# A graph layer, a linear-attention mixer and sixteen experts on one core: the experts' buffers moved, two additions moved to VectorE, one load moved

## The chip, the cores and the metric

The kernel runs on one core of a Trainium2 chip. The metric is device time in microseconds (us) of one execution. A core has five engines that run side by side, each through its own instructions in order: TensorE (PE, with its weight loads shown as PEld), VectorE (DVE), ScalarE (ACT), GpSimd (POOL) and SyncE (SP). Here SP does nothing but issue DMAs and load registers for them; POOL issues the indirect DMAs (gathers and scatters by a list of rows) beside additions of its own. All data is float32.

## The reference, cut to what matters

```python
xn = _layernorm(x)                                   # x: 3125 x 256
x = x + gnn(xn, edge_attr_3, src, dst, ...) + mix(xn, ...)
x = x + ffn(_layernorm(x), ...)

# gnn: 100000 edges
tmp = relu(concat(h[src], w) @ W1.T + b1)            # summed into the rows dst
h_lin = relu(concat(h, h_N) @ W2.T);  return h_lin / max(norm(h_lin), 1e-12)

# mix: 4 layers
h = layernorm(x);  x = x + linear_attn(h) 
h = layernorm(x);  x = x + (gelu(h @ W1 + b1) @ W2 + b2)

# ffn: 16 experts, the best 2 of each node
topk_vals, topk_idx = top_k(x @ gate_w + gate_b, 2);  topk_w = softmax(topk_vals)
h = relu(x @ w1[e] + b1[e]);  o = h @ w2[e] + b2[e]  # 256 -> 512 -> 256
y = x + sum_k topk_w[k] * o[topk_idx[k]];  return layernorm(y) * gamma + beta
```

## The kernel before, in words

The 3125 nodes are 25 tiles of 125 rows, in seven blocks (five of four tiles, one of three, one of two; `BLOCKS`, `NB` = 7). The running x of all nodes stays in SBUF as `xm`. The program has these stages:

1. The graph's edges and the first three mixer layers, interleaved, to about 1350 us.
2. The last mixer layer (from L1138). For each block `b`: `stage_f1` (first half), `stage_y(b+1)`, `stage_ln2(b+1)`, `add_update(b+1)`, `stage_yn(b-1)`, `stage_f1` (second half), `stage_g(b+2)`, `stage_yT(b-1)`, `stage_f2` (first pair of tiles), `stage_logits(b-1)`, `stage_t2(b+1)`, `stage_f2` (second pair), `stage_ranks(b-1)`, `stage_stats(b)`. `stage_ln2` normalizes a block into `xh` on DVE and then adds the bias `b2` to `xm` on POOL (L667). `add_update` loads the block's x into `xr` (SP), adds it to `xm` on POOL (L740), and then adds the normalized graph update to `xm` on DVE (L744). `stage_f2` adds the second product to `xm` on DVE (L700). `stage_yn` writes the experts' input of a block to the DRAM table `ynodes` (SP), and adds `beta` to `xm` on POOL (L1077). `stage_logits` and `stage_ranks` choose two experts for each node (DVE `lg`, `gate`, `sel`; PE `l_ps`, `rank_ps`), and eight scatters per block of four tiles (POOL, L1131) write each node into a slot of its expert in the DRAM table `slots`.
3. The first four expert tiles (`early`). They are full tiles of 256 slots that are known three blocks before the end of the layer. Their buffers lie in the memory of `hNT` and `qT`, which this layer no longer needs: `ew` (two sets of expert weights, written as `hNT<-ffn_w`), `ygT`, `yg` (the gathered rows, L140), `hs`, `o`. Their gathers are called for at b = NB - 2 (`e_nodes`), their products run between and behind the last block's stages, and their results are scattered into the DRAM table `outs` (L211).
4. The experts' phase (from L1215). Pools of SBUF are opened and closed like a stack; the new pools `big2`, `wts2` and `tmp2` take the place of the closed `big`, `wts` and `tmp`. `big` held `qT`, `hNT`, two `xh1`, `msum` and two `kmax`, in this order; `big2` holds `ogs` (51,200 bytes per partition), `gamma` and `eps`; `wts2` four weight buffers `ew` and six `yg`; `tmp2` `ids`, `ygT`, `hs`, `hb`, `o`. `run_tiles` goes through 33 tiles, 16 of them of 128 slots and 17 of 256, nearly in turn. For each tile: `load_slots` (SP: `ids<-slots`, L1241, some with an expert's number from a register), `load_weights` (SP: `ew<-ffn_w`, L147, 1.15 MB), `load_nodes` (POOL: `yg<-ynodes`, L140), `stage_t` (PE transposes L157, ACT copy L159), `stage_e1` (PE L167 or L175), `stage_ht` for small tiles, `stage_e2` (PE L204, DVE L208 and L209, POOL scatter L211). Loads of slots run six tiles ahead, weights and nodes three.
5. Two branches for tiles beyond these, and the output stage (from L1301): SP loads the results of all nodes from `outs` into `ogs` with 32 DMAs; PE sums each node's two rows, ACT and DVE normalize, DVE multiplies by `gamma` (L1341) and adds `xm` (L1342), POOL's queue stores.

What sets the order of an engine's instructions: in `tc.manual_schedule(engines=...)` the engines named keep the order of the program, and a scheduler orders the others by its own estimate of when each instruction is ready. In the first three layers these are PE, ACT and POOL; in the last layer PE and ACT (`in_order - {Pool}`); in `run_tiles` PE and ACT. So the order on SP, POOL and DVE in stages 2 to 4 is the scheduler's. It may also lift an instruction that stands behind the branches in the program over them, if nothing ties it to them: `eps` (L1303) is set before the experts' phase.

Of the kernel before, what the change touches and what calls it, by code (L numbers as in the profile page):

```python
# [8 lines left out]
F32 = mybir.dt.float32  # L9
# [8 lines left out]
D = 256  # L18
P = 128
TP = 125  # L20
# [35 lines left out]
def rows_bcast(ap, parts):  # L56

    return bass.AP(tensor=ap.tensor, offset=ap.offset, ap=[[0, parts], [1, ap.shape[-1]]])
# [7 lines left out]
def gps_layer(ctx: ExitStack, tc: tile.TileContext, a, out):  # L66
    nc = tc.nc
# [4 lines left out]
    def by_parts(queue, dst, src):  # L72

        for p in (slice(0, TP // 16 * 16), slice(TP // 16 * 16, TP)):
            queue.dma_start(dst[p], src[p])  # L75

    def by_tile(rows):

        return rows.rearrange("(p t) d -> p t d", t=NT)
# [28 lines left out]
    def rsqrt(dst, v, u):  # L108

        nc.vector.tensor_scalar(u.bitcast(I32), v.bitcast(I32), 1, None, op0=ALU.logical_shift_right)  # L110
        nc.vector.tensor_scalar(dst.bitcast(I32), u.bitcast(I32), -1.0, float(0x5f3759df),
                                op0=ALU.mult, op1=ALU.add)
        for _ in range(3):
            nc.vector.scalar_tensor_tensor(u, v, -0.5, dst, op0=ALU.mult, op1=ALU.mult)
            nc.vector.tensor_mul(u, u, dst)  # L115
            nc.vector.scalar_tensor_tensor(dst, u, 1.5, dst, op0=ALU.add, op1=ALU.mult)

    def finish_stats(r):
        rs = slice(r[0], r[-1] + 1)
        nc.vector.tensor_scalar(rs_v[:, rs], mv[:, rs, 1], EPS, None, op0=ALU.add)  # L120
        rsqrt(rstd[:, rs], rs_v[:, rs], rs_u[:, rs])

    def normalize(dst, src, t):
        nc.vector.tensor_scalar(dst, src, mv[:, t, 0:1], rstd[:, t:t + 1],
                                op0=ALU.subtract, op1=ALU.mult)
# [94 lines left out]
    with ExitStack() as ph:  # L220
        big = ph.enter_context(tc.tile_pool(name="big", bufs=1))
# [187 lines left out]
        NB = len(BLOCKS)  # L409
# [9 lines left out]
        def worked(columns, mark=None):  # L419


            nonlocal place
            if not spread or held:
                return
            place += columns * (NG + 1 + LEAD) / total
            while due and due[-1][0] <= place:
                _, kind, step, i = due.pop()
                if kind == 0 and mark is not None:
                    nc.gpsimd.tensor_copy(tick, mark)
                    mark = None  # L430
                step(i)
# [76 lines left out]
        def stage_stats(b):  # L508
            for t in BLOCKS[b]:
                stats(tmp, xm[:, t, :], t)  # L510
# [135 lines left out]
        def stage_y(l, b):  # L646
            for t0, o, n in pairs(b):
                ps = mm_tile("y_ps")[:TP].rearrange("p (i d) -> p i d", d=D)
                for i in range(n):
                    for c in range(KC):  # L650
                        nc.tensor.matmul(ps[:, i, :], qT[:, c, cols(t0 + i)], mo[:, c, :],  # L651
                                         start=(c == 0), stop=(c == KC - 1))
                xs = xm[:, t0:t0 + n, :]
                nc.vector.tensor_add(xs, xs, ps[:, :n, :])
                for t in range(t0, t0 + n):
                    stats(tmp, xm[:, t, :], t)
                worked(n * KC * D, xm[:1, t0, :1])

        def stage_ln2(b):
            r = BLOCKS[b]  # L660
            finish_stats(r)
            xh = tmp.tile([TP, BT, D], F32, name="xh")
            st["xh", b] = xh
            for i, t in enumerate(r):
                normalize(xh[:, i, :], xm[:, t, :], t)
            xs = xm[:, r[0]:r[-1] + 1, :]
            nc.gpsimd.tensor_add(xs, xs, b2[:TP, None, :].to_broadcast([TP, len(r), D]))  # L667

        def stage_t2(l, b):
            h2T = tmp.tile([P, KC, BT * TP], F32, name="h2T")  # L670
# [33 lines left out]
        def load_update(b):  # L704
            r = BLOCKS[b]
            n = len(r)
            xnT = tmp.tile([P, KC, BT * TP], F32, tag="hT", name="xnT", bufs=2)
            nc.sync.dma_start(xnT[:, :, :n * TP], xnT_d[:, :, cols(r[0], n)])
            hl = tmp.tile([TP, BT, D], F32, tag=("qs", "ek")[b % 2], name="hl")
            ss = tmp.tile([TP, 3, BT], F32, name="ss", bufs=2)  # L710
            st["update", b] = xnT, hl, ss
# [18 lines left out]
                                                   op1=ALU.mult, accum_out=ss[:, 0, i:i + 1])  # L730


        def add_update(b):
            r = BLOCKS[b]
            n = len(r)
            _, hl, ss = st.pop(("update", b))
            xr = tmp.tile([TP, BT, D], F32, tag="ekT", name="xr")
            by_parts(nc.sync, xr[:, :n, :], xv[:, r[0]:r[-1] + 1, :])
            xs = xm[:, r[0]:r[-1] + 1, :]
            nc.gpsimd.tensor_add(xs, xs, xr[:, :n, :])  # L740
            nc.vector.tensor_scalar(ss[:, 0, :n], ss[:, 0, :n], 1e-24, None, op0=ALU.max)
            rsqrt(ss[:, 1, :n], ss[:, 0, :n], ss[:, 2, :n])
            for i, t in enumerate(r):
                nc.vector.scalar_tensor_tensor(xm[:, t, :], hl[:, i, :], ss[:, 1, i:i + 1], xm[:, t, :],  # L744
                                               op0=ALU.mult, op1=ALU.add)
# [3 lines left out]
        def start_layer(l):  # L749
            nonlocal b2  # L750
            load(l, "Wo", "W1", "W2")
            b2 = tmp.tile([P, D], F32, name="b2")
            nc.sync.dma_start(b2, rows_bcast(a["mix_b2"][l], P))
# [384 lines left out]
        with tc.manual_schedule(engines=in_order - {mybir.EngineType.Pool}):  # L1138
            start_layer(last)
            load_update(0)  # L1140
            load_update(1)

            def worked(columns, mark=None):
                pass

            context(last, [lambda: stage_q(last, NB - 1), lambda: stage_g(0, slice(0, 1)),
                           lambda: stage_g(0, slice(1, 2)), lambda: stage_g(1, slice(0, 1))])
            stage_y(last, 0)
            stage_qT(last, NB - 1)
            stage_ln2(0)  # L1150
            add_update(0)
            stage_g(1, slice(1, 2))
            stage_t2(last, 0)
            stage_y(last, 1)
            for b in range(NB):
                stage_f1(last, b, range(0, NF // 2))
                if 0 < b < NB - 1:
                    stage_y(last, b + 1)
                if b + 1 < NB:
                    stage_ln2(b + 1)  # L1160
                    add_update(b + 1)
                if b == NB - 2:
                    for x in early:
                        e_nodes(x)
                if b > 0:
                    stage_yn(b - 1)
                stage_f1(last, b, range(NF // 2, NF))
                if b + 2 < NB:
                    load_update(b + 2)
                    stage_g(b + 2)  # L1170
                if b > 0:
                    stage_yT(b - 1)
                stage_f2(last, b, slice(0, 1))
                if b > 0:
                    stage_logits(b - 1)
                if b + 1 < NB:
                    stage_t2(last, b + 1)
                stage_f2(last, b, slice(1, 2))
                if b > 0:
                    stage_ranks(b - 1)  # L1180
                stage_stats(b)
                if b == NB - 3:
                    early_loads(BLOCKS[b][0])
            stage_yn(NB - 1)
            e_t(early[0])
            e_1(early[0])
            stage_yT(NB - 1)
            e_2(early[0], 0)
            stage_logits(NB - 1)
            e_t(early[1])  # L1190
            e_2(early[0], 1)
            stage_ranks(NB - 1)
            e_weights(early[2])
            e_1(early[1])
            for i in range(1, NFE):
                e_2(early[i], 0)
                if i + 1 < NFE:
                    e_t(early[i + 1])
                e_2(early[i], 1)
                if i + 2 < NFE:  # L1200
                    e_weights(early[i + 2])
                if i + 1 < NFE:
                    e_1(early[i + 1])
# [11 lines left out]
    with ExitStack() as ph:  # L1215
        big = ph.enter_context(tc.tile_pool(name="big2", bufs=1))
# [7 lines left out]

        ogs = big.tile([TP, K, NT, D], F32, name="ogs")
        gamma = big.tile([P, D], F32, name="gamma")
        nc.sync.dma_start(gamma, rows_bcast(a["ffn_gamma"], P))

        which_e, first, rest, loaded = [], [], [], set()

# [69 lines left out]

        ov = by_tile(out)  # L1301
        eps = big.tile([TP, 1], F32, name="eps")
        nc.vector.memset(eps, EPS)  # L1303
        ends = [1, 3, 7, 11, 15, 19, 23, NT]
        parts = [range(i, j) for i, j in zip([0] + ends, ends)]
# [110 lines left out]
```

## Time and profile before

| | us |
|---|---|
| median of 3 runs | 1956.14 (1951.93 to 1962.21) |
| the profiled execution | 1949.88 |
| its span, first to last instruction | 1948.2 |
| PE busy | 1808.2 (93%) |
| DVE busy | 1164.5 (60%) |
| POOL busy | 1117.7 (57%) |
| ACT busy | 749.0 (38%) |
| mean granted TensorE clock | 0.965 |
| last product of the first four expert tiles starts, ends | 1675.99, 1677.98 |
| first transposes of the experts' phase | 1691.08 |
| last product of the experts' phase ends | 1887.7 |
| output loads issued | 1897.95 to 1920.5 |

In the lines of the profile, a line begins with the engine (SPq is SP's queue) and names the line of the kernel, then output<-inputs by the program's names and the shape. Times are us from the start of the span. "<-" behind an idle time names what ended it; "issue" there means that the profile shows nothing that the engine waited for.

### The profile page before, as it was taken

To read this page: it belongs to the slowest core of one execution; us is meant where nothing else is said; L and a number is where in the kernel's file an instruction comes from. 1 tells how busy PE (TensorE), PEld (TensorE's weight loads), DVE (VectorE), ACT (ScalarE), POOL (GpSimd) and SP (SyncE) were. 2 spreads that over 40 slices of the span, in tenths; PEclk is the share of its full clock that TensorE was granted. 3 is DMA by queue.
4 is the path that set the end of the run, shared out by engine and by line. 5 is a ranking of instruction groups with operands and counts; after the bars stand their busy time and mean duration, and the time that the engine had idled before them with its cause. 6 is when DMAs were issued, how large, how long until landed. Compare 5 with 4: busy or idle time off the path is not lost. (4 is left out here: it accounts for less than half of the span.)

```text
span 1948.2 us, 28580 instructions
## 1 busy us (share of the span) xinstructions
PE 1808.2 (93%) x8965; PEld 1225.3 (63%) x8965; DVE 1164.5 (60%) x3727; ACT 749.0 (38%) x1352; POOL 1117.7 (57%) x1414
## 2 busy tenths in 40 slices
PE   6989999999989999999889999998899998799975
PEld 4865655666656566656555555666677777588862
DVE  7654666766665776666655666774546664233336
ACT  3532454444534444554233554443222232122222
POOL 1005788888828788888267888881113446355521
PEclk8998999999999999999889999999999999899997
DMA  6212333333513333334323333333211003577746
GB/s 173 91 52 68 97 107 103 103 102 106 150 52 102 95 103 104 106 101 125 90 77 88 102 103 105 103 108 95 91 41 27 20 17 109 182 266 277 268 146 196
DMA packets 95088, 216.64 MB, mean 111 GB/s; under 512 B 26760, under 2 KB 53391, under 8 KB 90192
## 3 DMA queue, kind: packets, MB, share of 16 engines
q0 software_dynamic: 45904, 121.36, 21.6%
q1 hardware_dynamic: 49024, 93.34, 15.0%
q8 instruction: 77, 1.26, 0.3%
q14 instruction: 83, 0.68, 0.1%
HBM read 192.20 MB, written 22.35 MB: 110 GB/s over the span
## 5 line engine op out<-in xcount | busy, mean ns | idle before, releaser
L348 POOL DMA_INDIRECT gat<-proj,src_i x784 | 760.1, 970 | 190.0 <-issue 142.3
L685 PE MATMUL f_ps<-h2T,ww 128*128 128x500 f32 (+2 forms) x896 | 369.5, 561 | 7.2 <-ACT h2T L442 6.2
L695 PE MATMUL f_ps<-ww,gT 128*125 128x256 f32 x1600 | 362.9, 382 | 0.1
L392 ACT ACTIVATE gat<-gat 128x512 f32<-128x512 f32 x392 | 239.2, 630 | 308.5 <-DVE gat L391 291.6
L391 DVE TENSOR_TENSOR gat<-gat,pw 128x512 f32<-128x512 f32 x392 | 250.6, 677 | 171.8 <-PE pw L386 156.6
L695 PEld LDWEIGHTS f_ps<-ww,gT 128*125 128x125 f32 x1600 | 294.2, 187 | 70.7 <-issue 21.5
L685 PEld LDWEIGHTS f_ps<-h2T,ww 128*128 128x128 f32 x896 | 169.5, 196 | 184.7 <-issue 130.2
L687 ACT ACTIVATE gT<-f_ps,ffb 128x500 f32<-128x500 f32 (+2 forms) x224 | 135.6, 632 | 139.3 <-PE f_ps L685 138.8
L667 POOL TENSOR_TENSOR xm<-xm,b 125x1024 f32<-125x1024 f32 (+2 forms) x28 | 59.6, 2129 | 137.2 <-DVE rs_u L115 57.0
L372 PE MATMUL pq<-gat,hot 128*32 128x256 f32 x1568 | 121.9, 388 | 9.1 <-ACT gat L392 8.7
L366 DVE TENSOR_TENSOR hNT<-hNT,win_ps 128x64 f32 x392 | 84.2, 215 | 72.4 <-PE win_ps L363 62.7
L386 PE MATMUL pw<-w1w,ea 8*128 8x512 f32 x784 | 121.0, 644 | 0.8 <-DVE qs L568 0.6
L1131 POOL DMA_INDIRECT slots<-rec,at x50 | 59.8, 1196 | 102.9 <-DVE rs_u L115 63.8
L700 DVE TENSOR_TENSOR xm<-xm,f_ps 125x512 f32<-125x512 f32 (+1 forms) x52 | 34.6, 666 | 133.9 <-PE f_ps L695 133.9
L598 PE MATMUL m_ps<-xh,ek 125*128 125x257 f32 x400 | 96.6, 394 | 5.4 <-ACT ek L584 5.4
L651 PE MATMUL y_ps<-mo,qT 128*125 128x256 f32 x400 | 98.9, 402 | 0.8 <-DVE mo L641 0.8
L561 PE MATMUL q_ps<-wwq,hT 128*125 128x256 f32 x400 | 94.5, 387 | 4.7 <-DVE gat L391 2.9
L211 POOL DMA_INDIRECT outs<-o,ids x50 | 49.5, 989 | 84.7 <-DVE o L209 83.6
L204 PE MATMUL e_ps<-ew,hs 128*128 128x256 f32 x400 | 97.2, 380 | 0.5 <-DVE o L208 0.3
L535 PE MATMUL k_ps<-hT,wwk 128*128 128x500 f32 (+2 forms) x224 | 92.6, 556 | 4.9 <-DVE hT L444 4.2
L651 PEld LDWEIGHTS y_ps<-mo,qT 128*125 128x125 f32 x400 | 77.9, 200 | 23.8 <-issue 5.7
L91 DVE BATCH_NORM_STATS2 bnst<-xm 125x6 f32<-125x256 f32 x225 | 88.7, 414 | 4.8 <-DMA xm<-x 2.8
(268 smaller groups left out, 2585.6 us busy)
## 6 DMA issues: line engine op xcount, KB each, us to landing
ew<-ffn_w SPq DMA_DIRECT2D x33, 1154.0 KB
gat<-proj,src_i POOLq DMA_INDIRECT x784
ww<-mix_W SPq DMA_DIRECT2D x8, 1024.0 KB
ea<-ea_g SPq DMA_DIRECT2D x98, 64.0 KB
hNT<-ffn_w SPq DMA_DIRECT2D x4, 1154.0 KB
ogs<-outs SPq DMA_DIRECT2D x10, 448.0 KB
xnT_d<-stage SPq DMA_DIRECT2D x5, 500.0 KB
xnT<-xnT_d SPq DMA_DIRECT2D x5, 500.0 KB
```

Of the source, the lines that this page charges most:

```text
L204: nc.tensor.matmul(ps[:, j, :], x["hs"][:, f, j * P:(j + 1) * P], x["w2"][:, f, :], start=(f == 0), stop=(f == NEF - 1))
L348: nc.gpsimd.indirect_dma_start(out=gats[-1][:, (j // SC) % 2, j % SC, :], out_offset=None, in_=proj, in_offset=bass.IndirectOffsetOnAxis(a ...
L372: nc.tensor.matmul(pq[s * W:(s + 1) * W, :], hot[:, s * SC + i, :], gats[s // 2][:, s % 2, i, :], start=(i == 0), stop=(i == SC - 1))
L386: nc.tensor.matmul(pws[s], ea[s * W:s * W + SC * 4, :], w1w[s * W:s * W + SC * 4, :], start=True, stop=True)
L391: nc.vector.tensor_add(msg, msg, pws[s])
L392: nc.scalar.activation(msg, msg, AF.Relu)
L561: nc.tensor.matmul(ps[:, i, :], hT[:, c, cols(o + i)], wt["Wq"][:, c, :], start=(c == 0), stop=(c == KC - 1))
L598: nc.tensor.matmul(ps, st["ek", b][:, i, c * P:(c + 1) * P], xh1s[b % 2][:, i, :], start=(i == 0), stop=(i == n - 1))
L651: nc.tensor.matmul(ps[:, i, :], qT[:, c, cols(t0 + i)], mo[:, c, :], start=(c == 0), stop=(c == KC - 1))
L685: nc.tensor.matmul(ps, wt["W1"][:, c, f * P:(f + 1) * P], st["h2T", b][:, c, :m], start=(c == 0), stop=(c == KC - 1))
L687: nc.scalar.activation(gT[:, f, :m], ps, AF.Gelu, bias=ffb[:, l, f:f + 1])
L695: nc.tensor.matmul(ps[:, i, :], st["gT", b][:, f, cols(o + i)], wt["W2"][:, f, :], start=(f == 0), stop=(f == NF - 1))
```

## The change

Three edits. `stage_ln2` and `add_update` get an argument for the engine that adds the bias `b2` and the block's x to `xm`; it is POOL as before, but DVE for the last block (`b + 2 == NB`). In `big2` a tile `room` of 2304 floats per partition (9,216 bytes) is laid out behind `gamma`; nothing reads or writes it, and all that is laid out after it lies so much higher. The load of `gamma` moves from the start of the experts' phase to the start of the output stage, behind the branches in the program.

```diff
-        def stage_ln2(b):
+        def stage_ln2(b, adder=nc.gpsimd):
...
-            nc.gpsimd.tensor_add(xs, xs, b2[:TP, None, :].to_broadcast([TP, len(r), D]))
+            adder.tensor_add(xs, xs, b2[:TP, None, :].to_broadcast([TP, len(r), D]))
...
-        def add_update(b):
+        def add_update(b, adder=nc.gpsimd):
...
-            nc.gpsimd.tensor_add(xs, xs, xr[:, :n, :])
+            adder.tensor_add(xs, xs, xr[:, :n, :])
...
                 if b + 1 < NB:
-                    stage_ln2(b + 1)
-                    add_update(b + 1)
+                    adder = nc.gpsimd if b + 2 < NB else nc.vector
+                    stage_ln2(b + 1, adder)
+                    add_update(b + 1, adder)
...
         gamma = big.tile([P, D], F32, name="gamma")
-        nc.sync.dma_start(gamma, rows_bcast(a["ffn_gamma"], P))
+        big.tile([P, 2304], F32, name="room")
...
         eps = big.tile([TP, 1], F32, name="eps")
+        nc.sync.dma_start(gamma, rows_bcast(a["ffn_gamma"], P))
         nc.vector.memset(eps, EPS)
```

## The prediction

> **What bounds the kernel now.** The page's first part gives TensorE (PE) 93% of the span, so only what makes PE wait, or run slowly, costs time:
>
> ```profile
> PE 1808.2 (93%) x8965; PEld 1225.3 (63%) x8965; DVE 1164.5 (60%) x3727; ACT 749.0 (38%) x1352; POOL 1117.7 (57%) x1414
> ```
>
> Next the waits of the stretch 1600 to 1700 us, which holds the end of the last mixer layer, the first four expert tiles and the start of the experts' phase (columns: total, times, longest, in us):
>
> ```profile
> PE ygT_ps L157 <- issue: 13.1, 1, 13.1
> DVE xm L744 <- POOL xm L740: 12.2, 1, 12.2
> ...
> POOL yg L140 <- DMA ids<-slots: 10.0, 1, 10.0
> ...
> PE rank_ps L1119 <- DVE sel L1104: 6.2, 2, 4.0
> ```
>
> PE has two holes: 13.1 us ahead of the experts' first transposes, 4.0 us ahead of a rank product. For the first I read the timelines of PE, SP and POOL around it (start, duration, work, idle time before and its releaser):
>
> ```profile
> 1675.99 1.99 PE L204 MATMUL e_ps<-hNT,qT 128*128 128x256 f32 x8 [0.52 <-DVE qT L208]
> 1691.08 0.66 PE L157 MATMUL ygT_ps<-ident,yg 128*128 128x128 f32 x2 [13.10 <-issue]
> ...
> 1703.20 1.88 PE L167 MATMUL e_ps<-ew,ygT 128*128 128x512 f32 x4
> ...
> 1714.65 1.88 PE L167 MATMUL e_ps<-ew,ygT 128*128 128x512 f32 x4
> ```
>
> ```profile
> 1664.34 2.01 SPq L1241 DMA_DIRECT2D ids<-slots  x3
> 1681.92 0.34 SPq L1227 DMA_DIRECT2D gamma<-ffn_gamma  x1
> 1682.31 2.32 SPq L147 DMA_DIRECT2D ew<-ffn_w  x3
> ```
>
> ```profile
> 1671.43 0.97 POOL L211 DMA_INDIRECT outs<-qT,ids  x1 [1.54 <-DVE qT L209]
> ...
> 1679.24 0.97 POOL L211 DMA_INDIRECT outs<-qT,ids  x1 [1.54 <-DVE qT L209]
> 1682.70 0.99 POOL L140 DMA_INDIRECT yg<-ynodes,ids  x1 [2.49 <-issue]
> ```
>
> SP issues nothing from 1666.35 to 1681.92, then gamma and at once the experts' weights; POOL's gathers `yg` start at the same moment. The DVE timeline says what let go:
>
> ```profile
> 1600.55 1.16 DVE L124 TENSOR_SCALAR xh<-xm,mv,rstd 125x256 f32<-125x256 f32 x2
> 1613.92 0.88 DVE L744 SCALAR_TENSOR_TENSOR xm<-hl,ss,xm 125x256 f32<-125x256 f32 x2 [12.22 <-POOL xm L740]
> ...
> 1681.99 0.06 DVE L1303 MEMSET eps<- 125x1 f32 x1 [3.03 <-DMA outs<-qT,ids]
> ```
>
> `eps`, in the same new pool as gamma, waited for the landing of the last scatter that reads `qT`, so that scatter, issued at 1679.24, frees pool `big`. The sizes agree: `big` holds 25,024+25,280+2x4,128+2,080+64 = 60,704 B per partition, the new `big2` only 51,200+1,024+32 = 52,256. The next pool (`wts2`: `ew`, `yg`) begins inside the old `big`, on `xh1`, whose readers ended long before. That it waited all the same means the wait goes by whole pools. `ids`, laid wholly over the old `tmp`, went out at 1664.34.
>
> For the second hole, PE's timeline and windows with the granted clock (busy by engine, PEclk, DMA share, GB/s):
>
> ```profile
> 1610.38 3.62 PE L695 MATMUL f_ps<-ww,gT 128*125 128x256 f32 x16
> 1617.99 0.43 PE L1119 MATMUL rank_ps<-sel,earlier 125*125 125x64 f32 x2 [3.99 <-DVE sel L1104]
> ```
>
> ```profile
> 1619.00:1623.00 4.00, 3.78 (x11) 3.05 (x11) 3.72 (x24) 2.11 (x3) 3.09 (x3) 0.57 0.39 108
> 1650.00:1653.00 3.00, 1.43 (x9) 1.03 (x8) 2.90 (x11) 0.69 (x2) 2.34 (x3) 1.00 0.04 1
> 1653.00:1657.00 4.00, 4.00 (x13) 3.22 (x12) 2.64 (x16) 0.47 (x1) 2.75 (x3) 0.57 0.77 264
> ...
> 1691.00:1698.00 7.00, 6.32 (x15) 3.40 (x16) 0.05 (x1) 1.57 (x3) 0.52 (x1) 0.52 0.99 395
> ```
>
> DVE stood 12.2 us behind the last block's additions, which POOL had put between its gathers and scatters. Behind them on DVE were `lg` and the chain to `sel`, for which PE waited. Each hole is followed by PE at about half clock.
>
> **Change, part 1: the buffers.** With `room` `big2` is 52,256+9,216 = 61,472 B, 768 more than `big`, so `wts2` begins past it and waits only for the old `wts` and `tmp`. Their last readers are the second f2 product of the last block and its statistics, by 1638.4. SP then goes from `ids` (end 1666.35) to the three weights. From the first such issue (1682.31) to the end of POOL's wait for the next `ids`, queued behind them (1697.48), was 15.2 us, so all three land by 1681.6, and the first needs less: its product began 10.0 us after its issue, so by 1676.4.
>
> PE can't start before the PSUM of the four tiles is read: DVE's last L208 runs 1678.02 to 1678.44, so 1678.6 instead of 1691.08, 12.5 us earlier. Then the clock. From the first transposes to the third tile's product took 1703.20-1691.08 = 12.1 us, against a full-clock period of 11.45. The first pair lacks the previous tile's e2 (2 x 1.73) and has about 1.1 us of transposes and copy and 0.75 of uncovered `hb` copy: 11.45-3.46+1.85 = 9.8. That is 2.3 more, 14.8 in all.
>
> Two deductions. The gathers: the early `ids` let POOL go 2.5 us after their issue (1606.68 to 1609.15), so `yg` issues at 1669, or at about 1673 behind the scatter of 1671.43. Under the weights' traffic it took 8.4 us to PE's start; the last early gather (1620.55) had landed when SP wrote `ynodes` at 1623.42, 2.9 us. So `yg` is ready between 1672 and 1681.4, PE up to 2.8 us late; I take 0.6, nearer to the early end, since the weights have a head start. The clock: a gap of about a microsecond remains. The rows show half clock (0.57) after a stretch with 1.43 of 3.00 us busy and no idle piece over 1.6 us. A half-clock stretch as in the row 1619 to 1623 costs 4.00 x 0.43 = 1.7; I take half of it, 0.85. [...] Part 1: -14.8+0.6+0.85 = -13.3, bounds -10.3 and -14.8.
>
> **Part 2: DVE adds.** No 125x512 addition of two SBUF tiles on DVE stands here; the nearest, gamma's product and the addition of x in the output stage, take 0.69 (L1341, L1342 at 512). Two are 1.4, on DVE that is idle from 1601.71 until f2's first PSUM at about 1608.5: hidden; uncovered, 1.4. The load of `xr` was issued at 1573.24. `lg` then runs at 1610.3 instead of 1615.3, `sel` ends by 1613, and PE goes from f2's end (1614.0) to the ranks: 3.99 saved. The half-clock stretch after the hole goes too, 1.7: -5.7. Bounds -4.0 (clock unchanged) and -6. POOL loses 2 x 1.29 us between its gathers, so it isn't late next: its next scatters could start at 1619.2, and their ranks are ready by 1617.2. Everything after is chained to these ranks and moves along.
>
> [...]
>
> **Part 3: gamma.** Its issue costs SP 0.34. Ahead of the 32 output loads (22.55 us, 0.70 each, which pace the output) it adds 0.34; if the scheduler lifts it over the branches, as it does with `eps`, nothing, since SP has little to issue until the first weight buffer comes free at about 1687. Its 128 KB at 269 GB/s delay the loads by 0.5 at most. I take +0.3.
>
> **Sum.** -13.3-5.7+0.3 = -18.7. The profiled execution took 1949.88 (span 1948.2), so 1931.2. The median of the runs is 6.3 above that execution: 1956.1-18.7 = 1937.4.
>
> **Rivals.**
> A. *POOL's order.* If the scheduler puts the fourth tile's gathers ahead of the last early scatters, POOL stands until those `ids`, behind three weights, are there (1681.6); two gathers later, at 1684.1, the scatter starts and lands 2.7 us on or more, and `eps`, still waiting for it, holds DVE to 1687 or 1690, while the first expert relu is wanted at 1683. Or the first gathers come after the last scatter (1680.5). For: POOL's order is the scheduler's, `eps` stood there before. Against: those `ids` are issued after the weights. Costs 6: 1943. Chance 0.13.
> B. *The buffers aren't freed*, because the wait doesn't go by pools as I read it. Only part 2 stays: 1956.1-5.4 = 1950.7. For: it is inferred from one wait. Against: `ids` went early. 0.10.
> C. *DVE adds bring nothing*, since the scheduler places them late on DVE or another wait follows: 1943. For: DVE's order is the scheduler's too. Against: it is idle there. 0.09.
> D. *Slower: SP's order.* Freed early, the experts' weights may be queued ahead of the weights of the third and fourth early tile (third issued at 1652.94, wanted at 1662.20). It decides when four loads, with the one whose expert comes from the tile list (ready at 1663.44), stand ahead. From about 1658.3 (both moved by part 2) three loads take 15.2 and two more 3.45 each (1.18 MB at the 343 GB/s of 1682.3 to 1697.5), 22.1 in all: 1680.4 against 1656.5 wanted. Early tiles end 23.9 later, at 1696.2, with a half-clock stretch at 1698; experts start at 1698.7 against 1691.1, less 2.3 for the faster first pair, +0.3 for gamma: +5.6, so 1961.7. Against: the third tile's weights are ready 10 us before the list. 0.06.
>
> **How the numbers follow.** My forecast has 0.62. A measurement tells about 0.5% (9.8 us) from no change. Faster by more: 0.61 of the forecast, 0.10 of A, 0.08 of C: 0.79. Within: the rest of A and C, most of B, half of D: 0.15. Slower: half of D and what I haven't seen: 0.06. The range runs from the full bounds (-14.8-6, 1935, less 5 for the scatter of the runs shown) to B: 1930 to 1950.
>
> **What would show it.** Right: SP issues `ew` within 3 us of the first `ids`, or even before; PE's hole before L157 `ygT_ps<-ident,yg` falls from 13.1 to under 3; PEclk is near 1.0 there; L744 no longer waits for POOL; the rank's 4.0 goes. `eps` still waits for the last scatter. Wrong: SP still stands until the last scatter lands (B), DVE stands at `eps` while PE waits (A), or L175 `e_ps<-hNT` waits for a DMA (D).

## The result, and the profile after

The changed kernel takes 1938.8 us (median of 6 runs, 1930.3 to 1941.2) where the kernel before takes 1953.4 beside it: ratio 0.9914, 95% interval 0.9885 to 0.9943, so 11 to 22 us faster. Run once more beside the kernel before (`after_again` below) it came to 1933.9 against 1954.2, ratio 0.9896 (0.9875 to 0.9918). The forecast was 1937.4, in a range of 1930 to 1950, from a gain of 18.7; the gains measured are 14.6 and 20.3.

The profiled execution is one of 1941.19 us with a span of 1939.5, only 8.7 below that of before. That difference is not the change's size. PE runs the same 8965 matmuls in the same order in both kernels, so each can be set beside its twin. The matmul that starts at 1577.49 before starts at 1585.03 after: this execution was 7.5 us late when it came to the first changed instruction, through more stretches at half clock in stages that are the same in both (49.5 us lost to half clock up to there, 41.0 before). Below, a time "from the mark" is counted from this matmul, and a gain is the difference of two such times.

| start of, us from the mark | before | after | gain | after_again |
|---|---|---|---|---|
| first rank product (last but two block) | 40.50 | 36.35 | 4.15 | 36.35 |
| second products of the last but one block | 50.55 | 44.62 | 5.93 | 44.62 |
| next rank product | 61.07 | 56.15 | 4.92 | 56.38 |
| last early tile's second products | 95.98 | 92.20 | 3.78 | 92.46 |
| first transposes of the experts' phase | 113.60 | 97.28 | 16.32 | 97.54 |
| third tile's first product | 125.72 | 106.96 | 18.76 | 107.22 |
| last matmul of the program | 351.44 | 334.10 | 17.34 | 333.87 |

The page's first part, and what is left on PE of the waits of 1590 to 1700 us (total, times, longest):

```profile
PE 1813.0 (93%) x8965; PEld 1227.6 (63%) x8965; DVE 1170.0 (60%) x3729; ACT 748.2 (39%) x1352; POOL 1114.6 (57%) x1412
```

```profile
PE rank_ps L1119 <- DVE sel L1104: 4.9, 2, 3.2
...
PE ygT_ps L157 <- issue: 0.6, 1, 0.6
```

The 13.1 us ahead of `ygT_ps` are 0.6, DVE's 12.2 at L744 are gone from the list, and `rank_ps` keeps 4.9, now ahead of another product. PE's timeline after (start, duration, work, idle time before and its releaser):

```profile
1621.38 0.33 PE L1119 MATMUL rank_ps<-sel,earlier 125*125 125x64 f32 x2
...
1641.18 0.65 PE L1119 MATMUL rank_ps<-sel,earlier 125*125 125x48 f32 x2 [3.23 <-DVE sel L1104]
...
1643.82 5.23 PE L175 MATMUL e_ps<-hNT 128*128 128x256 f32 x16 [0.69 <-ACT hNT L159]
...
1682.31 0.41 PE L157 MATMUL ygT_ps<-ident,yg 128*128 128x128 f32 x2 [0.56 <-issue]
1683.32 1.98 PE L167 MATMUL e_ps<-ew,ygT 128*128 128x512 f32 x4 [0.60 <-ACT ygT L159]
```

The first rank product now has no idle time before it. The second one waits longer than before (3.23, was 2.23), and the first early product behind it takes 5.23 where the same product later takes 3.62. At the boundary the transposes start 0.56 us behind the last early product (which ran from 1679.76 to 1681.76).

SP's queue after, and POOL's:

```profile
1641.12 0.36 SPq L147 DMA_DIRECT2D ew<-ffn_w  x1
...
1668.11 1.97 SPq L1244 DMA_DIRECT2D ids<-slots  x3
...
1705.74 0.36 SPq L1306 DMA_DIRECT2D gamma<-ffn_gamma  x1
```

```profile
1638.42 1.81 POOL L1077 TENSOR_TENSOR xm<-xm,beta 125x768 f32<-125x768 f32 x1
...
1673.96 0.99 POOL L140 DMA_INDIRECT yg<-ynodes,ids  x1 [0.30 <-PE e_ps L204]
...
1683.01 0.98 POOL L211 DMA_INDIRECT outs<-qT,ids  x1 [0.77 <-DVE qT L209]
```

The first experts' weight now goes out at 1641.12, 42 us before the last early scatter (1683.01), ahead even of the last two early tiles' weights (`hNT<-ffn_w`, from 1656.80); two more follow at 1670.98. The gathers `yg` stand between early scatters. gamma's load was lifted over the branches, as `eps` is, and goes out 23 us into the experts' phase.

### The profile page after: what moved, and what is told of

It reads as the page before. It is cut to its first block, busy times and chain, and to the rows that moved or that the text cites. A ratio compares the mean times of both kernels' runs of the same rounds, so it can differ in the third digit from the quotient of the medians.

```text
span 1939.5 us, 28572 instructions
## 1 busy us (share of the span) xinstructions
PE 1813.0 (93%) x8965; PEld 1227.6 (63%) x8965; DVE 1170.0 (60%) x3729; ACT 748.2 (39%) x1352; POOL 1114.6 (57%) x1412
## 5 line engine op out<-in xcount | busy, mean ns | idle before, releaser
L700 DVE TENSOR_TENSOR xm<-xm,f_ps 125x512 f32<-125x512 f32 (+1 forms) x52 | 34.7, 667 | 135.7 <-PE f_ps L695 132.6
```

## The experiments

Nine of the twelve kernels ran on three chips on which the kernel before takes 2194 to 2199 us, the last three on one with 1954. Nearly all of that difference lies ahead of the mark (at 1818 to 1830 us there, 1577 in the profile of before): up to there PE stands 195 to 207 us on those chips and 82 on the quicker ones, and loses 128 to 147 us to half clock against 31 to 50. What makes it is not shown. Each kernel is therefore set against the kernel before on its own chip, and the traces from the mark on.

| run | this, us | before, us | ratio, 95% interval | idle ahead of the first transposes, us |
|---|---|---|---|---|
| buffers_only | 2187.8 | 2199.1 | 0.9942 (0.9922 to 0.9963) | 1.21 |
| buffers_only_2 | 2185.9 | 2194.4 | 0.9949 (0.9922 to 0.9975) | 0.56 |
| adds_only | 2196.2 | 2199.1 | 0.9986 (0.9968 to 1.0004) | 12.91 |
| adds_only_2 | 2196.6 | 2194.4 | 0.9995 (0.9970 to 1.0019) | 12.86 |
| room_2104 | 2194.3 | 2199.1 | 0.9986 (0.9965 to 1.0007) | 13.51 |
| room_2112 | 2183.9 | 2199.1 | 0.9929 (0.9911 to 0.9946) | 0.56 |
| gamma_first | 2185.3 | 2197.1 | 0.9955 (0.9931 to 0.9980) | 0.56 |
| gamma_moved | 2196.6 | 2197.1 | 1.0001 (0.9974 to 1.0028) | 13.21 |
| beta_dve | 2182.0 | 2197.1 | 0.9926 (0.9898 to 0.9954) | 0.84 |
| after_again | 1933.9 | 1954.2 | 0.9896 (0.9875 to 0.9918) | 0.56 |
| late_rank | 1941.2 | 1954.2 | 0.9919 (0.9894 to 0.9944) | 3.43 |
| late_rank_beta | 1934.7 | 1954.2 | 0.9914 (0.9891 to 0.9937) | 2.54 |

### One part at a time

The buffers and gamma without the additions:

```diff
-                    adder = nc.gpsimd if b + 2 < NB else nc.vector
+                    adder = nc.gpsimd
```

> The buffer and gamma as in the changed kernel, the last block's two additions back on POOL. My theory: the two holes are separate, so PE's hole ahead of the experts' first transposes (13.1 us before, 0.6 after) stays under 1.5, DVE's 12 us wait at L744 and PE's 4.0 at the rank product come back, and the whole is 13 to 16 us faster than before, 2 to 4 us slower than the changed kernel. Rival, the additions did it (POOL, freed of 2.6 us, let its gathers and the weights go early): the hole stays above 8 us and the whole is less than 6 us faster than before.

The additions without the buffers:

```diff
-        big.tile([P, 2304], F32, name="room")
+        nc.sync.dma_start(gamma, rows_bcast(a["ffn_gamma"], P))
...
-        nc.sync.dma_start(gamma, rows_bcast(a["ffn_gamma"], P))
```

> The two additions on DVE alone, no room, gamma loaded at the start of the experts' phase as before. My theory: the 4.0 us wait at the rank product goes, and with what the next blocks give back the last early product comes 3 to 6 us earlier; the hole of 13 us ahead of the experts' first transposes stays within 2 us of 13, so the whole is 3 to 6 us faster than before. Rival, POOL's queue held the experts' weights: the hole falls below 5 and the whole is over 12 us faster.

The buffers bring 11 to 13 us of the chip's 15.6 (`room_2112`, next section): 0.9942 is 12.8 us of 2199. This is slightly below the 13 expected, and the hole is closed as expected. The additions bring 3.1 (interval -0.9 to 7.0), the lower end of what was expected and not clear of nothing, with the hole as it was. Both were run again on another of these three chips:

> [...] If the additions bring nothing (what is gained at the rank is given back on every chip), it is within 2 us of before.

> The buffers (and gamma) alone beside it. If the two parts simply add up to the changed kernel's 17 to 20 us: 13 to 16 faster than before. If the additions' part needs the buffers' or the other way round, the two gains sum to 3 us or more away from it.

There the additions bring nothing that can be measured (0.9995), the buffers 11.2, below the 13 expected; the two sum to 12.3. No run has one part alone on a quicker chip, so the split of the gain under "Why the prediction held" rests on traces of both parts together. The traces show where the additions' gain goes. PE's timelines of `adds_only` and of `buffers_only` over the same work:

```profile
1864.87 6.59 PE L685 MATMUL f_ps<-h2T,ww 128*128 128x250 f32 x30 [2.51 <-DVE xm L700]
...
1874.41 0.43 PE L238 MATMUL yT_ps<-ident,yb 125*128 125x125 f32 x2 [2.24 <-issue]
1875.85 8.86 PE L695 MATMUL f_ps<-ww,gT 128*125 128x256 f32 x32 [1.01 <-issue]
```

```profile
1865.42 0.43 PE L1119 MATMUL rank_ps<-sel,earlier 125*125 125x64 f32 x2 [4.20 <-DVE whichf L1099]
...
1875.38 2.32 PE L695 MATMUL f_ps<-ww,gT 128*125 128x256 f32 x10
```

With the additions on DVE the rank's 4.2 us are gone, but then PE stands 2.5, 2.2 and 1.0 us. The first of these waits is put down to DVE's L700, which itself started only at 1863.87, 2.4 us after the product that it reads had ended; for the other two the profile names nothing, and ACT stands from 1871.5 to 1873.9 in the same way. The granted clock is 1.00 meanwhile, and POOL and the DMAs go on (from 1871 to 1875.6 POOL is busy for 3.69 of 4.60 us, the DMA engines for 0.49 of the time). From the mark, the next block's second products start at 50.87 in `adds_only` and at 50.68 in `buffers_only`: the 4.2 us are gone again. The six other runs with DVE's additions on these chips stand 3.6 to 7.4 us in sum over the same work and reach the place at 50.7 to 52.7. On the quicker chips the same products follow with 0.17 us, and the place is reached at 44.62. So it is shown that the additions' gain is given back here; what makes the engines pause is not. Nor do the profile's DMAs tell it: of the queues that it lists as instruction queues, one moves a single packet (0.01 MB) in `adds_only` from 1855 to 1880 and in `adds_only_2` from 1861 to 1884, which hold the pauses, as one does in the like stretches of `after` (1616 to 1632) and `after_again` (1604 to 1620), which don't pause. So the cause stays open.

### What the weights waited for

A room that ends 32 bytes short of the old pool's end, and one that ends at it:

```diff
-        big.tile([P, 2304], F32, name="room")
+        big.tile([P, 2104], F32, name="room")
```

> The changed kernel with a room of 2104 floats in place of 2304: the new pool with the experts' weights then begins 32 B inside the old pool's memory, on a small tile that was last read some 300 us earlier. Theory of whole pools: those 32 B are enough, the first weight isn't issued before the last early scatter that reads qT is under way, the hole of PE ahead of the first transposes is again 10 us or more, and the whole is 12 to 16 us slower than the changed kernel. Rival, a new tile waits only for the old tiles that it lies on: the weights go out as in the changed kernel (first at about 1641), the hole stays under 1.5, and the time is within 2 us of the changed kernel's.

> The same with 2112 floats, 32 B more: the new pool begins exactly where the old one ends. Theory of whole pools: as the changed kernel within 2 us, hole under 1.5 us. Rival, that the room has to keep some distance or that other buffers' places matter (768 B further in the changed kernel): the hole comes back, 12 to 16 us slower than the changed kernel.

PE and SP of `room_2104`, then of `room_2112`:

```profile
1941.48 0.66 PE L157 MATMUL ygT_ps<-ident,yg 128*128 128x128 f32 x2 [13.51 <-DMA ew<-ffn_w]
```

```profile
1931.91 2.23 SPq L147 DMA_DIRECT2D ew<-ffn_w  x3
```

```profile
1927.05 0.41 PE L157 MATMUL ygT_ps<-ident,yg 128*128 128x128 f32 x2 [0.56 <-issue]
```

```profile
1885.83 0.36 SPq L147 DMA_DIRECT2D ew<-ffn_w  x1
```

Eight floats decide. With the new pool beginning 32 bytes inside the old one, on `kmax`, which no instruction had read for some 300 us, the weights go out together at 1931.91, 14 us behind the first `ids` (done at 1917.7) and 2.7 us behind the issue of the last early scatter (1929.23), and PE stands 13.5 us. Beginning at the old end, the first goes out at 1885.83, 27 us ahead of the first `ids` (1912.84), and PE stands 0.56. By time the two are 10.4 us apart (2194.3 and 2183.9, intervals of the ratios apart: 0.9965 and up, 0.9946 and below); from the mark to the last matmul 353.25 and 340.86, 12.4 apart. Expected were 12 to 16: the trace meets the lower end, the medians fall short of it. The first transposes are 12.5 apart. The theory of whole pools holds, and the rival, a wait for the tiles below alone, falls. The further 768 bytes of the change aren't needed for it: PE's idle time at the boundary is 0.56 with them and without.

### gamma

```diff
         gamma = big.tile([P, D], F32, name="gamma")
+        nc.sync.dma_start(gamma, rows_bcast(a["ffn_gamma"], P))
         big.tile([P, 2304], F32, name="room")
...
-        nc.sync.dma_start(gamma, rows_bcast(a["ffn_gamma"], P))
```

> The changed kernel with gamma's load left at the start of the experts' phase, where it was before. gamma lies in the pool that still covers the old pool's memory, so its load waits for the last early scatter's landing (about 1686). Theory A: the weights that matter are issued ahead of it on SP and nothing that PE needs soon stands behind it: hole under 1.5 us, within 2 us of the changed kernel. Theory B: it blocks SP's queue with weights behind it: the hole comes back in part or a wait for ew appears in the first tiles' products, 3 to 14 us slower than the changed kernel.

> gamma moved to the output stage and the additions on DVE, but no room. Theory A (the memory is the cause): the weights still wait for the last early scatter, hole of 12 to 14 us, as the kernel with the additions alone within 2 us. Theory B (gamma's load, which stood ahead of the weights on SP, was the cause of their wait): the weights go out earlier, hole under 5, within 3 us of the changed kernel.

SP's queue with gamma's load first and the room in place:

```profile
1936.76 0.34 SPq L1230 DMA_DIRECT2D gamma<-ffn_gamma  x1
1938.12 2.12 SPq L1245 DMA_DIRECT2D ids<-slots  x2
```

gamma waits for the old pool (1936.76) and the next `ids` wait behind it, but the four weights that PE needs first were out by 1925.3; from the mark the last matmul starts at 341.00, as in `room_2112` (340.86). In the trace theory A holds: the hole stays closed. The time alone doesn't settle it: 0.9955 is 9.9 us on this chip, and `room_2112`'s 0.9929, on another, 15.6, with intervals that overlap. Moving gamma without the room leaves the hole at 13.2 and the time at that of before (1.0001). So the move of gamma is neither needed nor enough.

### What took the additions' gain back

```diff
-            nc.gpsimd.tensor_add(xs, xs, beta[:TP, None, :].to_broadcast([TP, n, D]))
+            adder = nc.gpsimd if b < NB - 2 else nc.vector
+            adder.tensor_add(xs, xs, beta[:TP, None, :].to_broadcast([TP, n, D]))
```

> The changed kernel with the additions of beta of the last two blocks (L1077, 2.35 us each on POOL) on DVE too. Theory: in the changed kernel the gate at L1106 took 1.15 us in place of 0.15 while POOL's beta addition ran, and the second rank product waited 3.2 us for it; with the addition on DVE that lock is gone, but DVE has up to 2 us more of its own. If the addition falls into DVE's idle time, the second rank comes 1 us earlier and the whole is 1 to 2 us faster than the changed kernel. Rival: the additions stand ahead of the gate on DVE's own queue and delay it by as much as the lock did: within 1 us of the changed kernel, or up to 2 us slower.

This fell on a slower chip, where the pauses above had already moved DVE's gate out of POOL's way (in `adds_only` the gate starts at 1887.08, 6.0 us behind the end of POOL's beta addition, and takes 0.15 us; the rank product waits 2.23 with and without it), so it tells nothing of the lock. Its ratio, 0.9926, is not to be told from `room_2112`'s 0.9929. On a quicker chip the next three ran together:

> The changed kernel unchanged, beside the next two on one chip. The runs so far give buffers alone -12.7, a room that ends where the old pool ends with the additions -15.6; so 13 to 18 us faster than before. If the part of the additions is really nothing on this chip it is 11 to 14.

> The changed kernel with the second rank product of the trace (L1119 of block 5 of 0 to 6, for which PE waits 3.2 us in the changed kernel and 4 or so before) put behind the first early tile's transposes and first product on PE, which need nothing of it. Theory: PE's wait of 2.2 to 3.2 us there goes, and as the later steps depend on that rank only through the last blocks' slots, most of it is kept: 2 to 3 us faster than the changed kernel. Rival: the slots, and with them ids and the gathers of the experts' first tiles, come as much later, and PE waits for yg ahead of the first transposes instead: within 1 us, or slower by up to 3.

> late_rank with the additions of beta of the last two blocks on DVE as in beta_dve. If the lock on the gate (1.15 us in place of 0.15) and the wait at the rank are separate pieces of the path, 1 us faster than late_rank; if the rank is no longer waited for, the lock costs nothing any more and it is within 1 us of late_rank.

```diff
-                if b > 0:
+                if 0 < b < NB - 1:
                     stage_ranks(b - 1)
...
             e_1(early[0])
+            stage_ranks(NB - 2)
             stage_yT(NB - 1)
```

`after_again` was expected 13 to 18 us faster and is 20.3 (16 to 24). `late_rank` missed: its ratio is 0.9919 and not, at 2 to 3 us below the changed kernel's 0.9896, 0.988 to 0.989. The intervals of the two overlap; from the mark its last matmul comes at 335.28, 1.4 us behind that of `after_again` (333.87). PE's timeline of `late_rank` at the boundary:

```profile
1681.59 0.41 PE L157 MATMUL ygT_ps<-ident,yg 128*128 128x128 f32 x2 [3.43 <-DMA ew<-ffn_w]
1682.60 3.78 PE L167 MATMUL e_ps<-ew,ygT 128*128 128x512 f32 x4 [0.60 <-ACT ygT L159]
```

The wait at the rank product is gone (at 1646.21 it follows its neighbour without one), and from the mark the last early tile's second products come at 88.99, 3.5 us before those of `after_again` (92.46). On the way there it gives 1.67 us back in a wait for the third early tile's weights (2.63 in `late_rank_beta`), which the changed kernel doesn't have. The first `ids` go out later than in `after_again` (85.3 against 83.3), and the first `yg` only 1.0 earlier (88.4 against 89.4), so PE stands 3.43 us at the boundary, runs the next 4.4 us at 0.53 of the clock (the product that takes 1.98 in the changed kernel takes 3.78), and starts the third tile's first product at 109.14 instead of 107.22. So it is the rival, PE waiting at the first transposes, that the trace shows. The wait is put down to `ew`; the transposes read only `yg`, issued 8.5 us before, as long as in the kernel before (8.4 from 1682.70 to 1691.08), so I take it to be the gather.

The lock shows in the pair `late_rank`, `late_rank_beta`. DVE's gate of `late_rank`, then the same instruction (one line further down) of `late_rank_beta`:

```profile
1638.73 1.55 DVE L1106 TENSOR_TENSOR gate<-top 125x3 f32<-125x3 f32 x1
```

```profile
1630.49 0.15 DVE L1107 TENSOR_TENSOR gate<-top 125x3 f32<-125x3 f32 x1
```

1.40 us less with beta's addition on DVE, and ACT, whose next instruction waits for the gate, lets PE go 1.39 earlier (a wait of 1.60 at L175 for 2.99). At the boundary PE still waits 2.54 us. The third tile's first product starts at 107.05, 2.1 earlier than in `late_rank`, but the last matmul at 335.41, as there (335.28). `late_rank_beta` (1934.7) is not to be told from the changed kernel (1933.9), nor by its interval from `late_rank`, so none of these versions is shown to beat the changed kernel.

## Why the prediction held

**Part 1** was sized at -13.3, with bounds of -10.3 and -14.8, and brought 18.76-3.78 = 15.0. The first transposes came 12.5 us earlier relative to the early products, as worked out, and lie where the reading of the last PSUM tile by DVE lets them (L208, 1681.79 to 1682.22; the transposes start at 1682.31): 0.56 us behind the last early product, to the hundredth as in `after_again`, `room_2112`, `gamma_first` and `buffers_only_2`. From them to the third tile's first product it takes 9.7 us (12.1 before; 9.8 forecast). The two deductions, 0.6 for late gathers and 0.85 for a half-clock stretch, weren't needed: the clock is 1.00 there, and `yg` went out at 1673.96, 8.4 us ahead of the transposes. That was close: where PE plainly stood for the gathers, 7.5 us (`late_rank_beta`) to 8.9 (`room_2104`) passed from the issue of `yg` to the transposes. The sign for it, `ew` no later than 3 us behind the first `ids`, was met: the first weight went out 27 us ahead of them. The wait for whole pools, the step on which everything hung, is shown by 32 bytes.

`eps` still comes 3.4 us behind the last scatter's issue (1686.42), but the profile puts its wait down to ACT, so that sign says nothing.

**Part 2** was sized at -5.7. The second products of the last but one block came 5.93 earlier, which is 4.15 at the rank and 1.8 of half clock that fell away. So far it held. The step that failed is "Everything after is chained to these ranks and moves along", and with it "POOL ... isn't late next". 2.15 us were given back by the last early products, so the term is -3.8. POOL's queue is a chain of its own (`ids`, eight gathers, eight scatters, then beta's addition), and lost only the 2.6 us of the two additions taken from it, while PE and DVE came 5.9 earlier. So DVE's next gate ran into POOL's beta addition, which it had missed before by 2.2 us (1635.24 to 1637.49). DVE's timeline after:

```profile
1610.74 3.75 DVE L744 SCALAR_TENSOR_TENSOR xm<-hl,ss,xm 125x256 f32<-125x256 f32 x2
...
1639.10 1.15 DVE L1106 TENSOR_TENSOR gate<-top 125x3 f32<-125x3 f32 x1
```

The gate took 1.15 us (0.15 before) and ended with the addition, 1638.42+1.81 = 1640.23; the rank product waited 1.0 longer. The same lock on L744 (3.75 us, 0.88 before, under the beta addition from 1611.84 to 1614.19) lay under PE's second products and cost PE nothing. Four profiles have a gate that runs long, and each ends within 0.04 us of POOL's beta addition: 1.15 us to 1640.25 after (the addition to 1640.23), 1.39 to 1628.06 in `after_again` (1628.02), 1.55 to 1640.28 in `late_rank` (1640.24), and 1.94 to 1651.38 before, in the last block (1651.35). With beta's addition on DVE (`late_rank_beta`) it takes 0.15. The two moved additions, 0.69 us each after, weren't held. The rest, 1.15 us, went to the clock:

```profile
1641.00:1647.00 6.00, 5.14 (x16) 4.13 (x17) 3.97 (x27) 0.60 (x1) 2.37 (x2) 0.51 0.64 210
```

The half-clock stretch in which this window lies lasts 6.8 us; the one at this place before, from 1639.7, lasts 3.4. From the rank product on that is 5.7 us at half clock against 3.4, so 2.9 lost against 1.7.

**Part 3** was sized at +0.3 and cost nothing that shows: SP issues the load at 1705.74, in the middle of the experts' phase, by the scheduler's lifting that the prediction had named as the other case.

**The sum**: -3.8-15.0 = -18.8 at the third tile (forecast -18.7, with +0.3 for gamma in it), -17.3 at the last matmul, -16.2 at the end of the span. The two misses, 1.7 too little in part 1 and 1.9 too much in part 2, cancelled: that the sum comes within 0.1 of the forecast at the third tile is luck, though both mechanisms were there. What is lost again in the experts' phase and the output stage, 2.6 us, the runs don't settle: from the third tile to the last matmul the fourteen profiles take 225.6 to 228.4 us, from there to the end 18.8 to 22.1, and the profile of before lies near the low end of both. On the three slower chips the kernels whose hole is closed gain 10 to 16, mostly by the buffers; what the additions add there (15.6 against 12.8, with intervals that overlap) is not clear of nothing, and their gain goes into pauses.

## What to carry to other kernels

When stages share memory through stacked pools, look at where the next stage's first buffers begin: a few bytes of overlap with a pool still in use can hold back a whole prefetch (here 32 bytes cost 12.4 us), and unused bytes in between are a cheap way out. When a wait is removed from one engine's queue, ask which other queue has its own chain and doesn't move along; it is what the earlier work runs into next (here a gate of 0.15 us, which took 1.15 beside POOL's addition). And set two profiles side by side by the same instruction, not by their spans: here 7.5 of 16 us were hidden by a part that hadn't changed.

## What was not expected of the hardware

- Engines that pause together for 3.6 to 7.4 us in sum, mostly for nothing that the profile names, in the same place in seven profiles on three chips, and not (0.17 us) in the four profiles with the same additions where the kernel before takes 1954 us.
- How short a pause is followed by half clock. In `late_rank_beta` PE stood 1.60 us, within 4.40 us of which it was busy for 2.82, and then ran at 0.67:

```profile
1627.00:1631.40 4.40, 2.82 (x22) 2.44 (x20) 2.71 (x19) 0.69 (x2) 2.58 (x3) 1.00 0.09 2
1631.40:1636.60 5.20, 5.18 (x16) 4.29 (x17) 4.13 (x22) 0.47 (x1) 0.00 (x0) 0.67 0.78 206
```

  while the 0.56 and 0.60 us at the boundary after left it at 1.00 (1682 to 1692).
